# Score 1 moved beside the norms of a two-layer graph network kernel, and written into other PSUM banks

## The chip, the cores and the metric

The kernel runs on one core of a Trainium2 chip. The time is the device time of one execution in microseconds, from runs of the same program; the profile is of one execution. Engines are named as in the profile: PE is TensorE (matmul), DVE is VectorE, ACT is ScalarE, POOL is GpSimd, SP is SyncE, which here only issues DMAs.

## What is computed

128 graphs of 128 nodes with 512 features go through two layers, each with a residual and a normalisation ahead of it. The first layer weighs nodes by products of queries and keys, masked by the adjacency and divided by the norm of each row; the second is an attention with 8 heads of 64.

```python
    # layer 0
    q, k, v = h @ Wq.T, h @ Wk.T, h @ Wv.T
    rel = adjacency.T[None] * einsum('bnd,bmd->bnm', q, k)
    rel = rel / jnp.linalg.norm(rel, axis=2, keepdims=True)
    out = einsum('bnm,bmd->bnd', rel, v)
    # layer 1
    scores = einsum('bihd,bjhd->bhij', q, k) / sqrt(64)
    weights = softmax(scores + where(adj == 0, -1e9, 0), axis=-1)
    out = einsum('bhij,bjhd->bihd', weights, v)
    # around each layer
    h = maximum(layernorm(x), 0);  x = x + layer(h, adj, ...)
```

## The kernel before

The graphs are taken in 32 groups of four. One pass of the loop (g = 0 to 31) works on several groups at once: `m` is layer 0 of group g, `l` is layer 1 of group g - 1, `p` is layer 1 of the group before that, `f` is layer 0 of group g + 1 (loads, statistics, normalised rows), and `n` is layer 1 of group g being prepared. So each pass holds one whole layer 0 and one whole layer 1.

The order of everything is written by hand: strings of steps (`FIRST` for g = 0, `SECOND` for g = 1, `ORDER` for the 30 passes after, `LAST` behind the loop). A step such as `l.S1` calls the method `S(1)` of `l`. Each engine gets its instructions in the order in which the steps stand, and waits in that order; between engines only data dependencies and free buffers hold.

Steps that matter here:

- The linear maps are products of 512 x 512 matrices, each in seven smaller products (P1, P2, P5, P6, P3, P7, P4 in order of time) with sums of blocks in place of the eighth. Each small product is eight matmul instructions on PE (line 225) into one of three PSUM banks, called x, y and z. P1 writes x, and its result is copied out (r1). P2 writes y, and DVE adds r1 to it. P5 writes z (copied out as r5), P6 adds onto x (copied out as r2), P3 adds onto z, P7 onto x and P4 onto x again, each followed by an addition on DVE (line 249) or a copy. P3 may write z only when the copy of P5 has been read from it. In layer 0's V product the copies are on ACT; in layer 1's they add a bias on DVE (line 242).
- `m.R` (line 389) computes the four masked relations' products into an outputs' bank; `m.mask_rel` (DVE) multiplies them by the adjacency, `m.square` (ACT) squares them, `m.N` (PE, line 415) sums the squares with a matrix of ones, `m.norms` turns those sums by a transpose on DVE (line 424) and POOL takes the power -1/2. `m.O0` to `m.O3` (PE, line 429) multiply by the values, and `m.xO0` to `m.xO3` (DVE, line 435) scale by the norm and add to x.
- `l.S0` to `l.S3` (PE, line 460, with 64 rows of the array) compute the scores of the eight heads of one graph into `pss`, a pair of PSUM banks of which there is one. `l.mk` (DVE, lines 469 and 471) adds the mask and takes the negative maximum; `l.ex` (ACT, line 478) takes eight exponentials with sums and sends the block to DRAM on ACT's queue; `l.wr` fetches it back turned by blocks, four DMAs on SP's queue; `l.wt` (DVE, lines 491 and 493) takes a reciprocal and transposes inside the blocks. `l.A0` and `l.A1` (PE, line 577) multiply by the values.
- `n.stat` (DVE, lines 290 and 291) takes the statistics of x after layer 0, `n.inv` (POOL) turns them into scale and shift, `n.hn` (ACT, line 308) normalises and sends the rows to DRAM, `n.rd` (SP) fetches them, `n.T` (DVE, line 320) transposes: these are the inputs `h` of the next pass's products. `f.stat` and `f.inv` do the same for the next group's layer 0.

The PSUM pools: `ps_mm` has four banks for products, `ps_s` the one pair for scores, `ps_o` two banks with the tag `po` for outputs, for R and for N.

Of the kernel before, what the change touches and what calls it, by code (L numbers as in the profile page):

```python
# [9 lines left out]
F32 = mybir.dt.float32  # L10
AF = mybir.ActivationFunctionType
# [3 lines left out]
P = 128  # L15
G = 4
# [5 lines left out]
def kernel(  # L22
# [14 lines left out]
):  # L37
    nc = tc.nc
    B, N, D = x.shape
    assert N == P and B % G == 0  # L40
    KD = D // P
    H, HD = 8, 64
    NH = KD
    NG = B // G
# [8 lines left out]
    npool = ctx.enter_context(tc.tile_pool(name="npool", bufs=3))  # L53
# [3 lines left out]
    small = ctx.enter_context(tc.tile_pool(name="small", bufs=8))  # L57
# [4 lines left out]
    ps_s = ctx.enter_context(tc.tile_pool(name="ps_s", bufs=1, space=PSUM))  # L62
    ps_o = ctx.enter_context(tc.tile_pool(name="ps_o", bufs=2, space=PSUM))
# [122 lines left out]
    TB, BK = 4, 32  # L186

    def send_blocks(src, n: int, name: str):
        f = 8 * BK // n
        d = scratch.tile([n, P, TB, f], F32, tag=f"d{n}", name=f"d_{name}")  # L190
        nc.scalar.dma_start(d.rearrange("n p j f -> p n (j f)"), src.rearrange("p n j f -> p n (j f)"))
        return d
# [180 lines left out]
    class Layer0(Layer):  # L373
        n = 0

        def start(self):
            g = self.g
            self.gT = ppool.tile([P, KD, G * P], F32, tag="pgv", name=f"gT_{g}")
            self.v = ppool.tile([P, G, D], F32, tag="pv0", name=f"v0_{g}")
            self.po = {}  # L380
            self.G = Product(self, "a", self.gT, True, name=f"pg_{g}")
            self.V = Product(self, "v0", self.v, False, name=f"pv0_{g}")
# [27 lines left out]

        def N(self):

            pn = ps_o.tile([P, G, BK], F32, tag="po", name=f"pn_{self.g}")
            for c in range(TB):
                nc.tensor.matmul(
                    pn[c * BK : (c + 1) * BK, :, :], lhsT=ones, rhs=self.sq[:, c, :],
                    start=True, stop=True,
                )
            self.pn = pn

        def norms(self):
            self.rn = small.tile([P, G], F32, tag="rn", name=f"rn_{self.g}")
            sums = small.tile([P, G, BK], F32, tag="sums", bufs=1, name=f"sums_{self.g}")
            nc.vector.transpose(sums.rearrange("p b q -> p (b q)"), self.pn.rearrange("p b q -> p (b q)"))
            nc.gpsimd.tensor_tensor(self.rn, sums[:, :, 0], mhalf, ALU.pow)

        def O(self, b):
# [9 lines left out]
    class Layer1(Layer):  # L437
        n = 1

        def start(self):  # L440
            g = self.g
            self.qT = ppool.tile([P, NH, G * P], F32, tag="pq", name=f"qT_{g}")
            self.kT = ppool.tile([P, NH, G * P], F32, tag="pk", name=f"kT_{g}")
            self.Q = Product(self, "q", self.qT, True, bq_sb, name=f"pq_{g}")
            self.K = Product(self, "k", self.kT, True, bk_sb, name=f"pk_{g}")
            self.rs, self.wT, self.ps, self.nmax, self.po, self.e = {}, {}, {}, {}, {}, {}
            self.dw, self.uw, self.total, self.do, self.uo = {}, {}, {}, {}, {}

        def start_v(self):
# [3 lines left out]
        def S(self, b):  # L453
            g = self.g

            pss = ps_s.tile([P, 2, NH, P], F32, tag="ps", name=f"pss_{g}_{b}")
            for k in range(NH):
                for r in range(2):
                    rows = slice(r * HD, (r + 1) * HD)
                    nc.tensor.matmul(  # L460
                        pss[:, r, k, :],
                        lhsT=self.qT[rows, k, ts(b, P)], rhs=self.kT[rows, k, ts(b, P)],
                        start=True, stop=True,
                    )
            self.ps[b] = pss.rearrange("p r k j -> p (r k) j")

        def mk(self, b):
            g, sc = self.g, self.ps[b]
# [27 lines left out]
            )  # L496

        def mk_r(self, b, r):  # L500
            sc = self.ps[b][:, r * NH : (r + 1) * NH, :]
            nc.vector.tensor_tensor(sc, sc, mask[:, None, :].to_broadcast([P, NH, P]), ALU.add)
            if r == 0:
                self.nmax[b] = small.tile([P, H], F32, tag="nmax", bufs=2, name=f"nmax_{self.g}_{b}")
            nc.vector.tensor_reduce(
                self.nmax[b][:, r * NH : (r + 1) * NH], sc, AX.X, ALU.max, negate=True
            )
# [117 lines left out]
    SECOND = """  # L625
        l.Q.P1 l.sumA l.Q.P2 l.sumB l.K.P1 l.K.P2 l.Q.P5 l.Q.P6 f.load0 f.load1 l.Q.P3 l.K.P5 l.K.P6 l.Q.P7
        l.K.P3 l.K.P7 l.S0 l.mk0 f.load2 f.load3 l.Q.P4 l.K.P4 l.ex0 l.wr0 m.V.P1 f.stat0 f.stat1 f.inv0
        m.V.P2 l.S1 l.mk1 m.V.P5
        l.ex1 l.wr1 l.wt0 m.R m.mask_rel m.square f.stat2 f.stat3 f.inv1 m.V.P6 m.V.P3 m.N m.norms l.S2 l.mk2
        m.V.P7 l.ex2 l.wr2 l.wt1 m.O0 m.xO0 m.O1 m.xO1 n.stat0 n.stat1 n.inv0 m.V.P4 n.hn0 n.rd0 l.start_v l.V.P1  # L630
        m.O2 m.xO2 m.O3 m.xO3 n.stat2 n.stat3 n.inv1 l.V.P2 l.V.P5 n.hn1 l.V.P6 l.wt2
        n.rd1 l.V.P3 l.V.P7 n.T0 l.S3 l.A0 l.mk3 l.oc0 l.V.P4 l.ex3 n.T1 n.start
    """.split()
    ORDER = """
        l.Q.P1 p.rdo0 l.sumA l.Q.P2 p.wr3 m.hn0 l.sumB l.K.P1 m.rd0 l.K.P2 p.ot0 l.Q.P5 l.Q.P6 m.hn1 m.rd1
        l.Q.P3 l.Q.P7 p.wt3 m.T0 l.K.P5 l.K.P6 l.Q.P4 f.load0 f.load1 l.K.P3
        l.K.P7 m.T1 m.sumA m.sumB m.start m.G.P1 l.K.P4 m.G.P2 l.S0 p.A1 l.mk0 p.oc1 p.rdo1 m.G.P5 m.G.P6
        l.ex0 l.wr0 m.G.P3 m.V.P1 m.G.P7 p.ot1 m.V.P2 f.stat0 f.stat1 f.inv0 m.G.P4 l.S1 l.mk1 m.V.P5
        l.ex1 l.wt0 l.wr1 f.load2 f.load3 m.R m.mask_rel m.square m.V.P6 m.V.P3 m.N m.norms l.S2 l.mk2
        m.V.P7 l.ex2 l.wr2 l.wt1 m.O0 m.xO0 m.O1 m.xO1 n.stat0 n.stat1 n.inv0 m.V.P4 n.hn0 n.rd0 l.start_v l.V.P1  # L640
        m.O2 m.xO2 m.O3 m.xO3 n.stat2 n.stat3 n.inv1 l.V.P2 l.V.P5 n.hn1 f.stat2 f.stat3 f.inv1 l.V.P6 l.wt2
        n.rd1 l.V.P3 l.V.P7 n.T0 l.S3 l.A0 l.mk3 l.oc0 l.V.P4 l.ex3 n.T1 n.start
    """.split()
    LAST = """
# [19 lines left out]
    with tc.manual_schedule(engines={EN.PE, EN.SP, EN.Pool, EN.DVE, EN.Activation}):  # L664
        p, l, m = None, None, Layer0(0)
# [9 lines left out]
        f = Layer0(1)  # L675
# [3 lines left out]
        for g in range(NG):  # L679
            n = Layer1(g)  # L680
            if g:
                f = Layer0(g + 1) if g + 1 < NG else None
            run((FIRST, SECOND, ORDER)[min(g, 2)], p=p, l=l, m=m, n=n, f=f, w=Weights1())
            p, l, m = l, n, f
# [31 lines left out]
```

## Time and profile before

| | us |
|---|---|
| median of 3 runs | 2509.51 |
| lowest and highest | 2508.04, 2510.25 |
| the profiled execution | 2510.6 |
| its span | 2508.8 |
| ACT busy (share) | 1020.2 (41%) |
| exponentials, line 478, mean of one | 0.381 |
| mask and maximum over 1024, mean of one | 1.216 and 1.224 |
| transposes of weights, line 493, mean of one | 1.206 |
| statistics, line 290, mean of one | 0.671 |
| a score's matmuls, mean of one of 16 | 0.285 |
| TensorE clock granted | 0.999 |

The profiled execution is one of the same kind as the runs, with the span between its first and last instruction 1.8 us shorter than its time. "Mean of one" is an instruction's own length; instructions of one engine overlap at their ends, so the distance from start to start is shorter than that where they follow each other without a wait.

### The profile page before, as it was taken

Reading aid. Unit: us, or ns where it says so; the run is one execution under the profiler, and the core shown is the slowest. Engines: PE = TensorE matmul, PEld = TensorE weight load, DVE = VectorE, ACT = ScalarE, POOL = GpSimd, SP = SyncE. Lnnn points to the kernel's source line nnn. Section 1 sums busy time; section 2 is a strip of 40 time slices with the busy share of each in tenths; the row PEclk is TensorE's granted clock in tenths of the full one; section 3 lists DMA queues with packets and bytes.
Section 4 is the critical chain, followed back from the end, with each engine's and each line's share of the span. In section 5 each row is a group of like instructions: output and inputs, shape, how many; then the busy total and the mean of one; then the engine's idle time right before and its main releaser. Section 6 shows DMA issues by size and latency. Waiting matters only on the chain.

```text
span 2508.8 us, 40841 instructions
## 1 busy us (share of the span) xinstructions
PE 2488.8 (99%) x14672; PEld 2107.3 (84%) x14672; DVE 1709.0 (68%) x2485; ACT 1020.2 (41%) x3248; POOL 531.8 (21%) x944
## 2 busy tenths in 40 slices
PE   9999999999999999999999999999999999999998
PEld 6888888888888888888888888888888888888887
DVE  5566776666766667766677666676666776667766
ACT  3344343434434443434444343443443443444433
POOL 5111222121212212121122112121221212212211
PEclk9999999999999999999999999999999999999999
DMA  6255544555545555444555545554555644555543
GB/s 198 84 169 167 177 160 152 160 172 164 186 143 159 170 165 187 154 155 160 168 171 172 149 157 169 164 185 142 157 161 169 191 146 150 173 166 175 166 137 118
DMA packets 370475, 405.72 MB, mean 162 GB/s; under 512 B 29600, under 2 KB 286752, under 8 KB 370272
## 3 DMA queue, kind: packets, MB, share of 16 engines
q1 hardware_dynamic: 278992, 167.92, 24.8%
q10 hardware_dynamic: 70384, 166.74, 17.7%
q0 software_dynamic: 20896, 68.44, 8.3%
q8 instruction: 116, 1.90, 0.3%
q14 instruction: 87, 0.71, 0.1%
HBM read 204.80 MB, written 198.18 MB: 161 GB/s over the span
## 4 chain that ended last, share of the span: by engine, by line
PE 90%; DVE 4%; DMA 3%; ACT 1%; issue 1%; SPq 1%; POOL 0%; ACTq 0%; DVEq 0%
PE pv_x L225 15%; PE pg_x L225 9%; PE pk_x L225 8%; PE pq_x L225 8%; PE pv_z L225 8%; PE pss L460 5%; PE pg_z L225 5%; PE pq_z L225 5%; PE pr L389 4%; PE pk_z L225 4%; PE po L577 4%; PE pv_y L225 4%; PE po L429 4%; PE pg_y L225 2%; PE pk_y L225 2%; PE pq_y L225 2%
## 5 line engine op out<-in xcount | busy, mean ns | idle before, releaser
L478 ACT ACTIVATE e<-pss,nmax 128x128 f32<-128x128 f32 x1008 | 355.0, 381 | 281.3 <-PE pv_x L225 133.5
L612 POOL TENSOR_TENSOR xb<-xb,o 128x512 f32<-128x512 f32 x124 | 158.0, 1274 | 1212.6 <-DVE o L605 1211.1
L225 PE MATMUL pv_x<-wc_v,h 128*128 128x256 f32 x1280 | 301.6, 382 | 0.7 <-DVE pv_r L242 0.5
L225 PEld LDWEIGHTS pv_x<-wc_v,h 128*128 128x128 f32 x1280 | 239.4, 190 | 54.4 <-DVE v L249 11.7
L308 ACT ACTIVATE hn<-xb,shift,rstd 128x512 f32<-128x512 f32 x252 | 190.9, 807 | 172.5 <-POOL shift L300 170.6
L225 PE MATMUL pv_z<-wc_v,s 128*128 128x256 f32 x1024 | 245.1, 382 | 0.0
L320 DVE STREAM_TRANSPOSE h<-u_h 128x1024 f32<-128x1024 f32 x126 | 156.3, 1241 | 127.5 <-DMA u_h<-d_h 125.9
L478 ACT ACTIVATION_READ_ACCUMULATOR e<-pss,nmax 128x1 f32 x1008 | 221.2, 219 | 0.0
L225 PEld LDWEIGHTS pv_z<-wc_v,s 128*128 128x128 f32 x1024 | 191.8, 190 | 28.8
L225 PE MATMUL pv_x<-wc_v,s 128*128 128x256 f32 x768 | 184.9, 384 | 0.0
L225 PE MATMUL pq_x<-h,wc_q 128*128 128x256 f32 x768 | 181.9, 380 | 2.4 <-DVE h L320 2.4
L225 PE MATMUL pk_x<-h,wc_k 128*128 128x256 f32 x768 | 181.5, 379 | 0.0
L290 DVE BATCH_NORM_STATS2 st<-xb 128x6 f32<-128x512 f32 x256 | 171.9, 671 | 10.4 <-DMA xb<-in_x_dram 10.4
L588 ACT COPY oT<-po 128x512 f32<-128x512 f32 x124 | 72.7, 586 | 252.1 <-PE po L577 252.1
L493 DVE STREAM_TRANSPOSE wT<-u_w 128x1024 f32<-128x1024 f32 x126 | 151.9, 1206 | 32.6 <-DMA u_w<-d_w 32.6
L469 DVE TENSOR_TENSOR pss<-pss,mask 128x1024 f32<-128x1024 f32 x126 | 153.2, 1216 | 18.8 <-PE pss L460 15.0
L225 PEld LDWEIGHTS pq_x<-h,wc_q 128*128 128x128 f32 x768 | 145.3, 190 | 24.0 <-PE pv_x L225 2.1
L225 PEld LDWEIGHTS pk_x<-h,wc_k 128*128 128x128 f32 x768 | 145.8, 190 | 19.9
L225 PEld LDWEIGHTS pv_x<-wc_v,s 128*128 128x128 f32 x768 | 140.8, 190 | 20.6 <-issue 0.2
L460 PEld LDWEIGHTS pss<-kT,qT 64*128 64x128 f32 x2048 | 124.2, 187 | 39.4 <-issue 37.3
L471 DVE TENSOR_REDUCE nmax<-pss 128x8 f32<-128x1024 f32 x126 | 154.3, 1224 | 4.4
L460 PE MATMUL pss<-kT,qT 64*128 64x128 f32 x2048 | 148.7, 285 | 0.9 <-ACT e L478 0.5
(147 smaller groups left out, 4364.7 us busy)
## 6 DMA issues: line engine op xcount, KB each, us to landing
d_h<-hn ACTq DMA_DIRECT2D x126, 512.0 KB, 3.7
u_h<-d_h SPq DMA_DIRECT2D x504, 128.0 KB, 3.2
d_w<-e ACTq DMA_DIRECT2D x126, 512.0 KB, 2.6
u_w<-d_w SPq DMA_DIRECT2D x504, 128.0 KB, 3.0
xb<-in_x_dram POOLq DMA_DIRECT2D x124, 256.0 KB, 3.2
d_o<-oT ACTq DMA_DIRECT2D x62, 512.0 KB, 3.1
u_o<-d_o SPq DMA_DIRECT2D x248, 128.0 KB, 2.9
out_dram<-xb POOLq DMA_DIRECT2D x124, 256.0 KB, 3.1
```

Source lines behind the costliest of these rows:

```text
L225: nc.tensor.matmul(ps[:, m, :], lhsT=lhsT, rhs=rhs, start=first and m == 0 and k == 0, stop=k == 1, skip_group_check=True,)
L290: nc.vector.bn_stats(st, x_tiles[g, b])
L308: nc.scalar.activation(hn[:, r], x_tiles[g, b].rearrange("p (k j q) -> p j k q", j=TB, q=BK), AF.Relu, bias=self.shift[:, b : b + 1], scal ...
L320: nc.vector.transpose(half.rearrange("p k (t i) -> p t k i", i=BK), self.u.pop(i).rearrange("p t (k q) -> p t k q", q=BK),)
L389: nc.tensor.matmul(pr[:, b, :], lhsT=self.turned(k, b), rhs=self.gT[:, k, ts(b, P)], start=(k == 0), stop=(k == KD - 1),)
L429: nc.tensor.matmul(po, lhsT=self.rel[:, b, :], rhs=self.v[:, b, :], start=True, stop=True)
L460: nc.tensor.matmul(pss[:, r, k, :], lhsT=self.qT[rows, k, ts(b, P)], rhs=self.kT[rows, k, ts(b, P)], start=True, stop=True,)
L469: nc.vector.tensor_tensor(sc, sc, mask[:, None, :].to_broadcast([P, H, P]), ALU.add)
L471: nc.vector.tensor_reduce(self.nmax[b], sc, AX.X, ALU.max, negate=True)
L478: nc.scalar.activation(e[:, :, i, :], sc[:, i, :].rearrange("p (j q) -> p j q", q=BK), AF.Exp, bias=nmax[:, i : i + 1], accum_out=self.tot ...
L493: nc.vector.transpose(self.wT[b].rearrange("p h (t i) -> p t h i", i=BK), self.uw.pop(b).rearrange("p t (h q) -> p t h q", q=BK),)
L612: nc.gpsimd.tensor_tensor(xb, xb, o.rearrange("p k t q -> p (k t q)"), ALU.add)
```

## The change

Scores 1 (`S1`, in the passes that have a layer 0 beside them) no longer go to the pair `pss` but to two tiles of the outputs' pool `ps_o`, heads 0 to 3 of the kernel's order in one and 4 to 7 in the other. Mask, maximum and exponentials of scores 1 and 2 are done in halves: `mkA1`, `exC1`, `mkB1`, `exD1`, and the same for 2. `N` takes no outputs' bank any more, but the first part of the V product's bank y.

In the order, `S1` moves from ahead of `m.V.P5` to between `m.V.P6` and `m.N`, with `S2` behind `N`; R comes earlier by that much; `m.V.P3` moves behind `S2`. `wt0` stands ahead of R without a score before it. `wr1` is issued later, `wt1` goes from ahead of `xO0` to behind `xO3`. In `ORDER`, `f.stat2` moves to ahead of `l.V.P1` and `f.stat3` to ahead of `l.V.P2`; before, both stood behind `l.V.P5`.

```diff
         def N(self):
-            pn = ps_o.tile([P, G, BK], F32, tag="po", name=f"pn_{self.g}")
+            pn = self.V.ps["y"].rearrange("p m (b q) -> p (m b) q", q=BK)[:, 0:G, :]
...
         def S(self, b):
-            pss = ps_s.tile([P, 2, NH, P], F32, tag="ps", name=f"pss_{g}_{b}")
+            if b == 1 and g < NG - 1:
+                half = [ps_o.tile([P, NH, P], F32, tag="po", name=f"pso_{g}_{r}") for r in range(2)]
+            else:
+                pss = ps_s.tile([P, 2, NH, P], F32, tag="ps", name=f"pss_{g}_{b}")
+                half = [pss[:, r] for r in range(2)]
+                self.ps[b] = pss.rearrange("p r k j -> p (r k) j")
+            self.half_s[b] = half
...
-                        pss[:, r, k, :],
+                        half[r][:, k, :],
...
+        def ex_h(self, b, r):
+            g, sc, nmax = self.g, self.half_s[b][r], self.nmax[b]
+            if r == 0:
+                self.total[b] = small.tile([P, H], F32, tag="total", bufs=4, name=f"total_{g}_{b}")
+                self.e[b] = npool.tile([P, TB, H, BK], F32, tag="e", name=f"e_{g}_{b}")
+            e = self.e[b]
+            for k in range(NH):
+                i = r * NH + k
+                nc.scalar.activation(
+                    e[:, :, i, :], sc[:, k, :].rearrange("p (j q) -> p j q", q=BK), AF.Exp,
+                    bias=nmax[:, i : i + 1], accum_out=self.total[b][:, i : i + 1],
+                )
+            if r == 1:
+                self.dw[b] = send_blocks(self.e.pop(b).rearrange("p j h q -> p (j h q)").rearrange(
+                    "p (n j f) -> p n j f", n=1, j=TB), 1, f"w_{g}_{b}")
...
         def mk_r(self, b, r):
-            sc = self.ps[b][:, r * NH : (r + 1) * NH, :]
+            sc = self.half_s[b][r]
...
     ORDER = """
...
-        l.ex0 l.wr0 m.G.P3 m.V.P1 m.G.P7 p.ot1 m.V.P2 f.stat0 f.stat1 f.inv0 m.G.P4 l.S1 l.mk1 m.V.P5
-        l.ex1 l.wt0 l.wr1 f.load2 f.load3 m.R m.mask_rel m.square m.V.P6 m.V.P3 m.N m.norms l.S2 l.mk2
-        m.V.P7 l.ex2 l.wr2 l.wt1 m.O0 m.xO0 m.O1 m.xO1 n.stat0 n.stat1 n.inv0 m.V.P4 n.hn0 n.rd0 l.start_v l.V.P1
-        m.O2 m.xO2 m.O3 m.xO3 n.stat2 n.stat3 n.inv1 l.V.P2 l.V.P5 n.hn1 f.stat2 f.stat3 f.inv1 l.V.P6 l.wt2
+        l.ex0 l.wr0 m.G.P3 m.V.P1 m.G.P7 p.ot1 m.V.P2 f.stat0 f.stat1 f.inv0 m.G.P4 m.V.P5
+        l.wt0 f.load2 f.load3 m.R m.mask_rel m.square m.V.P6 l.S1 m.N l.S2 l.mkA1 m.norms l.exC1 l.mkB1 l.exD1
+        l.wr1 m.V.P3 l.mkA2 l.exC2 m.V.P7 l.mkB2 l.exD2 l.wr2 m.O0 m.xO0 m.O1 m.xO1 n.stat0 n.stat1 n.inv0
+        m.V.P4 n.hn0 n.rd0 l.start_v f.stat2 l.V.P1 m.O2 m.xO2 m.O3 m.xO3 l.wt1 n.stat2 n.stat3 n.inv1 f.stat3
+        f.inv1 l.V.P2 l.V.P5 n.hn1 l.V.P6 l.wt2
         n.rd1 l.V.P3 l.V.P7 n.T0 l.S3 l.A0 l.mk3 l.oc0 l.V.P4 l.ex3 n.T1 n.start
     """.split()
```

`SECOND` changes in the same way, but keeps `f.stat2 f.stat3 f.inv1` ahead of `m.V.P6`.

More of the change, by code (lines that the diff above doesn't have):

```diff
@@ L416, in N @@
                     pn[c * BK : (c + 1) * BK, :, :], lhsT=ones, rhs=self.sq[:, c, :],
-                    start=True, stop=True,
+                    start=True, stop=True, skip_group_check=True,
                 )
-            self.pn = pn
         def norms(self):
@@ L423, in norms @@
             sums = small.tile([P, G, BK], F32, tag="sums", bufs=1, name=f"sums_{self.g}")
-            nc.vector.transpose(sums.rearrange("p b q -> p (b q)"), self.pn.rearrange("p b q -> p (b q)"))
+            nc.vector.transpose(sums.rearrange("p b q -> p (b q)"), self.V.ps["y"].rearrange("p m h -> p (m h)")[:, 0:P])
             nc.gpsimd.tensor_tensor(self.rn, sums[:, :, 0], mhalf, ALU.pow)
@@ L446, in start @@
             self.rs, self.wT, self.ps, self.nmax, self.po, self.e = {}, {}, {}, {}, {}, {}
+            self.half_s = {}
             self.dw, self.uw, self.total, self.do, self.uo = {}, {}, {}, {}, {}
@@ L464, in S @@
                     )
-            self.ps[b] = pss.rearrange("p r k j -> p (r k) j")
         def mk(self, b):
@@ L496, in wt, with exC, exD @@
             )
+        def ex_h(self, b, r):
[13 more added lines that the diff above has]
+                    "p (n j f) -> p n j f", n=1, j=TB), 1, f"w_{g}_{b}")
+        def exC(self, b):
+            self.ex_h(b, 0)
+        def exD(self, b):
+            self.ex_h(b, 1)
         def mk_r(self, b, r):
-            sc = self.ps[b][:, r * NH : (r + 1) * NH, :]
+            sc = self.half_s[b][r]
             nc.vector.tensor_tensor(sc, sc, mask[:, None, :].to_broadcast([P, NH, P]), ALU.add)
@@ L627 @@
         l.K.P3 l.K.P7 l.S0 l.mk0 f.load2 f.load3 l.Q.P4 l.K.P4 l.ex0 l.wr0 m.V.P1 f.stat0 f.stat1 f.inv0
-        m.V.P2 l.S1 l.mk1 m.V.P5
-        l.ex1 l.wr1 l.wt0 m.R m.mask_rel m.square f.stat2 f.stat3 f.inv1 m.V.P6 m.V.P3 m.N m.norms l.S2 l.mk2
-        m.V.P7 l.ex2 l.wr2 l.wt1 m.O0 m.xO0 m.O1 m.xO1 n.stat0 n.stat1 n.inv0 m.V.P4 n.hn0 n.rd0 l.start_v l.V.P1
-        m.O2 m.xO2 m.O3 m.xO3 n.stat2 n.stat3 n.inv1 l.V.P2 l.V.P5 n.hn1 l.V.P6 l.wt2
+        m.V.P2 m.V.P5 l.wt0 m.R m.mask_rel m.square f.stat2 f.stat3 f.inv1 m.V.P6 l.S1 m.N l.S2 l.mkA1 m.norms l.exC1
+        l.mkB1 l.exD1 l.wr1 m.V.P3 l.mkA2 l.exC2 m.V.P7 l.mkB2 l.exD2 l.wr2 m.O0 m.xO0 m.O1 m.xO1 n.stat0 n.stat1
+        n.inv0 m.V.P4 n.hn0 n.rd0 l.start_v l.V.P1 m.O2 m.xO2 m.O3 m.xO3 l.wt1 n.stat2 n.stat3 n.inv1 l.V.P2
+        l.V.P5 n.hn1 l.V.P6 l.wt2
         n.rd1 l.V.P3 l.V.P7 n.T0 l.S3 l.A0 l.mk3 l.oc0 l.V.P4 l.ex3 n.T1 n.start
@@ L637 @@
         l.K.P7 m.T1 m.sumA m.sumB m.start m.G.P1 l.K.P4 m.G.P2 l.S0 p.A1 l.mk0 p.oc1 p.rdo1 m.G.P5 m.G.P6
-        l.ex0 l.wr0 m.G.P3 m.V.P1 m.G.P7 p.ot1 m.V.P2 f.stat0 f.stat1 f.inv0 m.G.P4 l.S1 l.mk1 m.V.P5
-        l.ex1 l.wt0 l.wr1 f.load2 f.load3 m.R m.mask_rel m.square m.V.P6 m.V.P3 m.N m.norms l.S2 l.mk2
-        m.V.P7 l.ex2 l.wr2 l.wt1 m.O0 m.xO0 m.O1 m.xO1 n.stat0 n.stat1 n.inv0 m.V.P4 n.hn0 n.rd0 l.start_v l.V.P1
-        m.O2 m.xO2 m.O3 m.xO3 n.stat2 n.stat3 n.inv1 l.V.P2 l.V.P5 n.hn1 f.stat2 f.stat3 f.inv1 l.V.P6 l.wt2
+        l.ex0 l.wr0 m.G.P3 m.V.P1 m.G.P7 p.ot1 m.V.P2 f.stat0 f.stat1 f.inv0 m.G.P4 m.V.P5
[3 more added lines that the diff above has]
+        f.inv1 l.V.P2 l.V.P5 n.hn1 l.V.P6 l.wt2
         n.rd1 l.V.P3 l.V.P7 n.T0 l.S3 l.A0 l.mk3 l.oc0 l.V.P4 l.ex3 n.T1 n.start
```

## The prediction

> **What bounds the kernel now.** I read the page's first two parts, then the waits of TensorE, then the order of time on PE and DVE in one group of the loop.
>
> ```profile
> span 2508.8 us, 40841 instructions
> PE 2488.8 (99%) x14672; PEld 2107.3 (84%) x14672; DVE 1709.0 (68%) x2485; ACT 1020.2 (41%) x3248; POOL 531.8 (21%) x944
> PE pq_x L225 <- DVE h L320: 2.4, 3, 1.1
> PE pv_x L225 <- DVE pv_r L242: 0.5, 3, 0.2
> ```
>
> TensorE sets the end: 99% busy, almost nothing waited for. The other engines count only where they come late for one of its steps. Ends on PE are modelled, so I measure its steps from start to start. A product of eight matmuls takes 1.727 us wherever nothing disturbs it. Compared with the shortest time of the same step, all starts of the trace together hold 11.2 us of excess: some 10 us of it in the loop, at three places: Q.P1 waiting for `h`, Q.P5 for the addition behind Q.P2, and V.P7 of layer 1 for its bias copy on DVE. A group without a wait lasts 76.73 us (N to N), the mean one 77.1.
>
> This is PE in the pass g = 15 (the first columns are start and length):
>
> ```profile
> 1177.03 1.16 PE L460 MATMUL pss<-kT,qT 64*128 64x128 f32 x16
> 1178.12 1.99 PE L225 MATMUL pv_z<-wc_v,s 128*128 128x256 f32 x8
> 1179.95 3.73 PE L389 MATMUL pr<-gT,h 128*128 128x128 f32 x32
> 1183.52 1.89 PE L225 MATMUL pv_x<-wc_v,s 128*128 128x256 f32 x8
> 1185.25 1.89 PE L225 MATMUL pv_z<-wc_v,s 128*128 128x256 f32 x8
> 1187.07 0.43 PE L415 MATMUL pn<-sq,ones 128*32 128x128 f32 x8
> 1187.43 1.16 PE L460 MATMUL pss<-kT,qT 64*128 64x128 f32 x16
> 1188.52 1.99 PE L225 MATMUL pv_x<-wc_v,s 128*128 128x256 f32 x8
> 1202.42 1.89 PE L225 MATMUL pv_z<-wc_v,s 128*128 128x256 f32 x8
> 1204.45 1.99 PE L225 MATMUL pv_x<-wc_v,h 128*128 128x256 f32 x8
> ```
>
> The reader should see two things. V.P5 after S1 takes 1.83 us to the next start, V.P3 before N 1.82, both instead of 1.727: going to a narrow form costs 0.09 and coming back 0.10, while N to S2 costs nothing. And V.P7 of layer 1 (last line) starts 2.03 after V.P3: 0.31 of waiting. DVE shows for what:
>
> ```profile
> 1188.64 1.23 DVE L469 TENSOR_TENSOR pss<-pss,mask 128x1024 f32<-128x1024 f32 x1 [0.47 <-PE pss L460]
> 1193.38 1.25 DVE L493 STREAM_TRANSPOSE wT<-u_w 128x1024 f32<-128x1024 f32 x1 [1.55 <-DMA u_w<-d_w]
> 1194.55 1.36 DVE L435 SCALAR_TENSOR_TENSOR xb<-po,rn,xb 128x512 f32<-128x512 f32 x2
> 1201.52 0.68 DVE L242 TENSOR_TENSOR pv_r<-pv_z,bv_sb 128x512 f32<-128x512 f32 x1
> 1203.73 0.66 DVE L242 TENSOR_TENSOR pv_r<-pv_x,bv_sb 128x512 f32<-128x512 f32 x1
> ```
>
> From S2 on DVE runs without a break, but for 1.55 us before wt1, where it waits for a DMA. The copy of V.P6 starts at 1203.73 and PE goes on at 1204.45, 0.72 later. The copy of V.P5, at 1201.52, was due by 1202.42 - 0.72 = 1201.70 for V.P3. This queue has little to spare, and the change works on it.
>
> [...] The trace: a mask and maximum over 1024 takes 1.26 + 1.14 = 2.40 us from start to start; in the last stage, where they go in halves, 0.73 + 0.61 = 1.34, so two halves 2.68: 0.14 for each instruction added.
>
> **The change, part by part.**
>
> *Narrow steps together.* One pair of switches goes in each of the 31 groups that have a layer 1: 31 x 0.197 = 6.1 us off. S1 to N isn't in the trace; N to S2 and S0 to the outputs of layer 1 (64*128 to 128*64) show no cost, so 0, at most another 0.1 (3 us).
>
> *R, and S1 in the outputs' banks.* Without S1 ahead and its switches, V.P6 would start at 1183.52 - 1.09 - 0.20 = 1182.23, S1 at 1184.05, N 1185.14, S2 1185.50, V.P3 1186.59, V.P7 1188.42; from O0 on all is 0.20 earlier. S1's second bank is that of R, free when mask_rel has read it: R ends at 1182.2, mask_rel takes 0.7, and wt0 ahead of it has its data 7.2 us after ex0's issue at 1171.93, so 1179.2. S1 waits for nothing, by over 1 us. N in V's y bank: y was read at 1177.6, the square is done near 1183.8. O0 and O1 need the halves read by exC1 and exD1, about 1188.0 and 1189.6, against 1190.15. S2 no longer waits for score 1 at all. Cost 0.
>
> *Halves.* Two more instructions for each of two scores on DVE, 0.28 each. ACT does the same exponentials, 0.34 us apart.
>
> *DVE up to V.P5's copy.* V.P3's addition can't start before its product ends: 1186.59 + 2.03 = 1188.62 (a product's addition starts 1.93 after the product, 0.10 more behind a score). By then mkA1, norms, mkB1 are done (1185.12 + 1.34 + 0.22 + 1.34 = 1188.02). From there nothing is waited for: V.P3's addition 0.61, mkA2 1.34, V.P7's addition 0.60, mkB2 1.34: xO0 at 1192.51 (before 1194.55). xO0, xO1 1.29; two statistics of n 1.61; f.stat2, new here, 0.81; V.P1's copy 0.57; xO2, xO3 1.32; wt1 0.11 + 1.12; two statistics 1.61; f.stat3, new here, 0.81; V.P2's addition 0.57. Sum from xO0: 9.82, so V.P5's copy starts at 1202.33. PE could start V.P3 at 1202.22 and gets it at 1202.33 + 0.72 = 1203.05: **a new wait of 0.83**, and 0.10 more, as the step after each such wait in the trace is 0.104 longer. 29 groups have an f in this order: 29 x 0.93 = 27.0 us. In the group run by SECOND, f's statistics stand elsewhere, and the last has no f: 1.6 us less on DVE, no wait.
>
> *wt1 later.* Its data: mkB1 done 1188.1, exD1 until 1189.6, issue about 1189.75, last block 7.28 later (median of this trace; longest 11.7): 1197.0, turn at 1198.2. Now this fetch runs beside score 2's writing; the fourth weights, which share the DMA, take 8.6. So 0 to 0.4 of wait in a typical group; I take 0.05, 1.5 us. On SP, wr1 and wr2 go ahead of rd0: wr2's issue is at about 1194.1, as before; rd0 needs hn0, 2 us earlier than before. rd0 also needs the buffer that wt1 frees, at 1199.3, before hn0's rows have landed (1202.4). Cost 0.
>
> *Waits that go.* hn0 comes 2 us earlier, so h, mk3, ex3 and Q's copies do too, against 0.6 more time on PE. The largest wait for h is 1.21, for qT 0.36. V.P7's goes, since its copy follows V.P5's by 0.6. I take 9.5 of 10 us off.
>
> Sum: -6.1 + 27.0 + 1.5 - 9.5 = **+12.9 us**. The profiled execution took 2510.6 around its span of 2508.8, the median run 2509.5: 2522.
>
> **Rivals.** (a) *DVE comes in time*: the copy of V.P5 is 0.83 earlier than I add up, or V.P3 doesn't wait for it. For it: xO0 is 2 us earlier, and this wait isn't in the trace before. Against: V.P7 waits for a copy in the same way, and every duration is measured. It gives 2509.5 - 6.1 - 9.5 = 2494. It decides for a faster kernel where the wait is below 0.2 us. (b) *The sum is right and wt1 comes late as well*: DVE has no slack left, so each 0.1 us of DMA delay costs 2.9 us; with 0.6 instead of 0.05, 2538. (c) *Half the wait*: 0.4 instead of 0.83, if additions start earlier than I take it; 2509.5 - 6.1 - 9.5 + 29 x 0.5 + 1.5 = 2510, no change. Slower by what can be told begins at a wait of 0.56.
>
> **Numbers.** Forecast, slower by a wait at layer 1's V.P3: 0.62 (2514.6 to 2534). (b) 0.13. (c) 0.09. (a) 0.16. What a measurement of this kernel can tell from no change is 0.2%, 5 us. Faster 0.16, same 0.09, slower 0.75. The likeliest's own range, from waits of 0.5 to 1.3, is 2511 to 2535; the range 2505 to 2535 takes in (c) and leaves (a) and the far part of (b) out.
>
> **What would show it.** Right: S1, N, S2 in a row with V.P6's next start at 1.82 and V.P3's at 1.83; a wait of PE for `pv_r` (L242) before `pv_z` in nearly every group; none left for `h` and `qT`; xO0 5.9 us behind V.P3's start. Wrong: no such wait, or one ended by a DMA before wt1, or PE waiting before S1 or the outputs.

## The result and the profile after

| | before | after |
|---|---|---|
| median, us (5 runs each) | 2509.04 | 2567.50 |
| lowest and highest | 2507.39, 2510.25 | 2563.59, 2568.77 |
| ratio, 95% interval | 1 | 1.0231 [1.0220, 1.0243] |
| profiled execution, its span | 2510.6, 2508.8 | 2563.6, 2561.8 |
| a pass of the loop, N to N, median of 29 | 76.91 | 78.65 |

The change makes the kernel 2.3% slower: 58 us, where 12.5 was forecast (2522 against 2509.5). The direction is right, the size is wrong, and the time lies outside the forecast's range.

First the page of the kernel after:

```profile
span 2561.8 us, 40938 instructions
PE 2493.8 (97%) x14672; PEld 2107.2 (82%) x14672; DVE 1727.8 (67%) x2609; ACT 1030.2 (40%) x3248; POOL 531.5 (21%) x944
```

And its waits of TensorE (who waits for whom: us in total, times, longest):

```profile
PE po L429 <- ACT v L233: 27.9, 32, 1.1
PE pv_z L225 <- DVE pv_r L242: 21.8, 29, 1.3
...
PE pso L467 <- DVE rel L398: 2.3, 1, 2.3
```

TensorE's busy time has hardly changed; two waits have appeared that stand in nearly every pass, and one that stands in one pass. The second of these lines is the forecast one: V.P3 of layer 1 waiting for V.P5's bias copy, 29 times. The first was not forecast: O2 waiting for ACT's copy of V.P4. This is one pass on PE (g = 14; start and length first, the wait in brackets):

```profile
1130.76 1.89 PE L225 MATMUL pv_x<-wc_v,s 128*128 128x256 f32 x8
1132.58 1.16 PE L467 MATMUL pso<-kT,qT 64*128 64x128 f32 x16
1133.67 0.43 PE L416 MATMUL pv_y<-sq,ones 128*32 128x128 f32 x8
1134.03 1.16 PE L467 MATMUL pss<-kT,qT 64*128 64x128 f32 x16
1135.12 1.99 PE L225 MATMUL pv_z<-wc_v,s 128*128 128x256 f32 x8
...
1140.40 3.62 PE L225 MATMUL pv_x<-wc_v,h 128*128 128x256 f32 x16
1144.87 1.98 PE L429 MATMUL po<-v,rel 128*128 128x512 f32 x4 [0.86 <-ACT v L233]
...
1152.74 1.99 PE L225 MATMUL pv_z<-wc_v,s 128*128 128x256 f32 x8 [0.70 <-DVE pv_r L242]
```

S1, N and S2 stand in a row and cost what they should: 1.82 from V.P6 to S1, 1.09 and 0.36 between them, nothing for S1 to N, 1.83 from V.P3 to V.P7. From V.P4's start to O2's are 4.47 us where two products take 3.45: a wait of 1.02. The bracket says 0.86, because it counts from the modelled end; I keep to starts. V.P3 waits 0.86 by its start. What comes before O2 is on DVE and ACT:

```profile
1135.35 0.67 DVE L530 TENSOR_TENSOR pso<-pso,mask 128x512 f32<-128x512 f32 x1
1136.05 0.69 DVE L533 TENSOR_REDUCE nmax<-pso 128x4 f32<-128x512 f32 x1
...
1137.83 0.69 DVE L530 TENSOR_TENSOR pss<-pss,mask 128x512 f32<-128x512 f32 x1
...
1139.16 0.68 DVE L249 TENSOR_TENSOR v<-pv_x,pv_r 128x512 f32<-128x512 f32 x1
1140.87 0.70 DVE L530 TENSOR_TENSOR pss<-pss,mask 128x512 f32<-128x512 f32 x1 [1.03 <-ACT e L513]
1142.21 1.40 DVE L435 SCALAR_TENSOR_TENSOR xb<-po,rn,xb 128x512 f32<-128x512 f32 x2
...
1152.00 0.68 DVE L242 TENSOR_TENSOR pv_r<-pv_z,bv_sb 128x512 f32<-128x512 f32 x1
```

The second half of score 1, `pso` at 1135.35, goes on while ACT takes the exponentials of the first (from 1135.28). The second half of score 2, `pss` at 1140.87, waits 1.03 us for the exponentials of its first half. The halves of score 1 are two tiles, those of score 2 two halves of one. On ACT, score 1 (first line) and score 2:

```profile
1136.33 0.38 ACT L513 ACTIVATE e<-pso,nmax 128x128 f32<-128x128 f32 x1
...
1140.37 0.37 ACT L513 ACTIVATE e<-pss,nmax 128x128 f32<-128x128 f32 x1
...
1142.33 0.37 ACT L513 ACTIVATE e<-pss,nmax 128x128 f32<-128x128 f32 x1 [1.49 <-DVE nmax L533]
...
1143.87 0.33 ACTq L191 DMA_DIRECT2D d_w<-e  x1
1144.23 0.59 ACT L233 COPY v<-pv_x 128x512 f32<-128x512 f32 x1 [0.40 <-PE pv_x L225]
```

ACT idles 1.49 us in the middle of score 2, does four exponentials and issues a DMA, and only then copies V.P4, whose product ended near 1142.1 (V.P4 starts at 1140.40, a product takes 1.73). O2 starts at 1144.87, when that copy is done, 0.64 behind the copy's start. In the kernel before, in the pass of the prediction, the copy stood behind exponentials and a DMA issue too, but started 0.95 ahead of O2 (1195.52):

```profile
1194.57 0.59 ACT L233 COPY v<-pv_x 128x512 f32<-128x512 f32 x1 [0.45 <-ACT e L478]
```

So it had about 0.3 us to spare there.

The maxima of both halves (`nmax`) also lie in one tile, in SBUF and in columns of their own. There nothing is serialised: DVE writes those of score 1's second half from 1136.05, while ACT still reads the first half's for its last exponential at 1136.33. So a shared tile does not always make a wait; here it was the two-bank tile in PSUM (the 1.03 us above).

The third wait is the one of the pass g = 1. On DVE:

```profile
106.76 1.25 DVE L499 STREAM_TRANSPOSE wT<-u_w 128x1024 f32<-128x1024 f32 x1 [5.79 <-DMA u_w<-d_w]
107.93 0.65 DVE L398 TENSOR_TENSOR rel<-pr,adj_sb 128x512 f32<-128x512 f32 x1
```

And on PE:

```profile
108.64 1.16 PE L467 MATMUL pso<-kT,qT 64*128 64x128 f32 x14 [2.27 <-DVE rel L398]
```

In `SECOND` wt0 comes sooner behind ex0, DVE waits 5.79 us for its data, mask_rel stands behind it, and the second bank of S1 is still R's: PE stops after the first two matmuls of S1.

An account of PE's starts over the whole profiled executions, each step's time to the next start against the shortest time of the same step:

| | forecast, us | measured, us |
|---|---|---|
| narrow steps together, 31 x 0.197 | -6.1 | -6.1 |
| V.P3 for V.P5's copy, 29 passes, with the longer step behind | +27.0 | +29.5 |
| of that, wt1's data late | +1.5 apart | within the 29.5 |
| old waits (11.2 before; 3.5 left) | -9.5 | -7.7 |
| O2 for V.P4's copy, 31 x 1.04 and 31 x 0.10 | 0 | +35.5 |
| S1 in the pass g = 1 | 0 | +2.8 |
| sum | +12.9 | +54.0 |

The spans differ by 53.0. Nearly all of the error stands in one line, that of O2. This tells where TensorE stood still; what each cause is worth, the experiments tell.

### The profile page after: what moved, and what is told of

Its sections match the earlier page's. It is cut to its first block, busy times and chain, and to the rows that moved or that the text cites. A ratio compares the mean times of both kernels' runs of the same rounds, so it can differ in the third digit from the quotient of the medians.

```text
span 2561.8 us, 40938 instructions
## 1 busy us (share of the span) xinstructions
PE 2493.8 (97%) x14672; PEld 2107.2 (82%) x14672; DVE 1727.8 (67%) x2609; ACT 1030.2 (40%) x3248; POOL 531.5 (21%) x944
## 4 chain that ended last, share of the span: by engine, by line
PE 78%; DVE 14%; ACT 3%; DMA 2%; issue 2%; SPq 0%; DVEq 0%; POOL 0%; ACTq 0%
PE pg_x L225 9%; PE pv_x L225 9%; PE pk_x L225 8%; PE pq_x L225 8%; PE pv_z L225 7%; PE pg_z L225 5%; PE po L605 4%; PE pq_z L225 4%; PE pr L389 4%; PE pk_z L225 4%; PE pss L467 4%; DVE st L290 4%; DVE xb L435 3%; PE pv_y L225 2%; PE pg_y L225 2%
## 5 line engine op out<-in xcount | busy, mean ns | idle before, releaser
L484 ACT ACTIVATE e<-pss,nmax 128x128 f32<-128x128 f32 x512 | 180.3, 383 | 43.7 <-DVE nmax L477 33.9
L429 PE MATMUL po<-v,rel 128*128 128x512 f32 x256 | 123.6, 605 | 27.9 <-ACT v L233 27.9
L633 DVE TENSOR_TENSOR o<-o,rs 128x512 f32<-128x512 f32 x124 | 124.5, 1004 | 4.3
L297 POOL TENSOR_SCALAR rstd<-mv 128x2 f32<-128x2 f32 x128 | 28.4, 222 | 465.6 <-DVE mv L291 460.9
L225 PE MATMUL pg_z<-s,wc_a 128*128 128x256 f32 x512 | 124.1, 385 | 0.0
L225 PE MATMUL pq_z<-s,wc_q 128*128 128x256 f32 x512 | 121.4, 380 | 1.4 <-DVE qT L249 1.4
```

The lines of the kernel that those rows point to most:

```text
L225: nc.tensor.matmul(ps[:, m, :], lhsT=lhsT, rhs=rhs, start=first and m == 0 and k == 0, stop=k == 1, skip_group_check=True,)
L429: nc.tensor.matmul(po, lhsT=self.rel[:, b, :], rhs=self.v[:, b, :], start=True, stop=True)
L484: nc.scalar.activation(e[:, :, i, :], sc[:, i, :].rearrange("p (j q) -> p j q", q=BK), AF.Exp, bias=nmax[:, i : i + 1], accum_out=self.tot ...
L633: nc.vector.tensor_tensor(heads, heads, self.rs.pop(b).rearrange("p (r k) -> p k r", r=2)[:, :, :, None].to_broadcast([P, NH, 2, HD]), ALU ...
```

## The experiments

Two theories. **A**: mkB2's wait for exC2, made by the tile that the halves share, delays exD2 and the copy and so O2; V.P3's wait is DVE's queue; the two lie on linked chains. **B**: ACT is late by itself (halves, the copy's place), and each wait adds its own time. Ratios are to the kernel before, run beside them on the same chip; its median there was 2506.4 to 2507.1.

**1. Tiles of their own for the halves.**

```diff
-                pss = ps_s.tile([P, 2, NH, P], F32, tag="ps", name=f"pss_{g}_{b}")
-                half = [pss[:, r] for r in range(2)]
+                half = [ps_s.tile([P, NH, P], F32, tag=f"ps{r}", name=f"pss_{g}_{b}_{r}") for r in range(2)]
```

> The two halves of every score lie in two PSUM tiles of one bank each instead of one tile of two banks (scores 0 and 3 therefore also take mask and maximum in halves, 0.28 us more on DVE each). Theory A (mkB2 on DVE waits 1.03 us for the exponentials exC2 only because both halves are one tile; this makes exD2 and the copy behind V.P4 late and O2 waits 1.02 + 0.10 us on PE): the wait of DVE before the second half of score 2 goes, O2's wait goes, V.P3's wait of 0.86 stays, because PE and DVE both come 1.1 us earlier; 31 x 1.12 = 35 us less, about 2533. Theory B (ACT is late by itself, with halves and the copy's place in its queue): O2 still waits, at least 0.7 us, and the time stays above 2550.

Measured 2538.4, ratio 1.0124 [1.0109, 1.0140]. In one pass DVE takes the second half of score 2 and xO0 without a wait:

```profile
1056.41 0.69 DVE L526 TENSOR_TENSOR pss<-pss,mask 128x512 f32<-128x512 f32 x1
...
1057.74 1.40 DVE L435 SCALAR_TENSOR_TENSOR xb<-po,rn,xb 128x512 f32<-128x512 f32 x2
```

xO0 starts 7.42 us behind N instead of 8.54, O2 waits for nothing, and a pass has a median of 77.53 us instead of 78.65. V.P3's wait stays at 0.80. That is theory A, and B is out: ACT has the same exponentials and copies in the same order and is in time. The typical pass gains the 1.12 us that were forecast, but the whole gains 27 us by the ratios and not 35. The mean of the passes is 77.97: with DVE earlier wt1's data come 1.2 to 2.1 us late in four of them, and in three places behind waits of 1.96 us or more TensorE's granted clock is 0.50, for 13.7 us in all, with 0.996 in the mean of the execution (last section). The wait of 1.03 came from the tile: with the order as it was and a half to each bank in both kernels, the edit takes it to zero.

**2. f.stat2 and f.stat3 back behind l.V.P5**, as before the change.

```diff
-        m.V.P4 n.hn0 n.rd0 l.start_v f.stat2 l.V.P1 m.O2 m.xO2 m.O3 m.xO3 l.wt1 n.stat2 n.stat3 n.inv1 f.stat3
-        f.inv1 l.V.P2 l.V.P5 n.hn1 l.V.P6 l.wt2
+        m.V.P4 n.hn0 n.rd0 l.start_v l.V.P1 m.O2 m.xO2 m.O3 m.xO3 l.wt1 n.stat2 n.stat3 n.inv1
+        l.V.P2 l.V.P5 n.hn1 f.stat2 f.stat3 f.inv1 l.V.P6 l.wt2
```

> Only f.stat2 and f.stat3 go back behind l.V.P5, as in the kernel before; all else is the changed kernel. Theory A (V.P3's wait is DVE's queue, which these two made 1.62 us longer ahead of V.P5's copy): the wait of 0.86 + 0.10 at V.P3 goes in all 29 passes, O2's wait stays at 1.02, so 28 us less, about 2539. Rival (the copy is late because of the wait before mkB2 alone, or because wt1's data are late): V.P3 still waits, and less than 10 us is gained.

Measured 2551.2, ratio 1.0177 [1.0162, 1.0192]; a pass takes 78.04. V.P3's standing wait is gone (3 times left), O2's is the same to 0.01. But 14 us are gained by the ratios, not 28: V.P7 now waits 0.263 in 30 passes, with 0.104 for the step behind it, for V.P6's copy, which these statistics now precede. These 11 us are most of what is missing; the wait moved by one product, and I had overlooked that end.

**3. exD2 behind V.P4's copy.**

```diff
-... l.mkB2 l.exD2 l.wr2 m.O0 ... m.V.P4 n.hn0
+... l.mkB2 m.O0 ... m.V.P4 l.exD2 l.wr2 n.hn0
```

> Only exD2 and wr2 go behind V.P4's copy in the order, so that the copy no longer stands behind them on ACT. Theory A (DVE's queue from V.P3's addition to V.P5's copy sets the pass, and O2's wait lies inside it): O2's wait of 1.02 goes and V.P3's grows from 0.86 to about 2.0; the time stays at 2567 within 4 us. Theory B (the two waits are independent and add up): 31 x 1.12 = 35 us less, about 2533.

Measured 2562.5, ratio 1.0224 [1.0208, 1.0239], where the changed kernel had 1.0231: the same. A pass takes 78.64, as before this edit. The waits of TensorE in this run:

```profile
PE pv_z L225 <- DVE pv_r L242: 53.3, 31, 1.8
...
PE po L429 <- ACT v L233: 0.7, 1, 0.7
```

O2's wait is left in one pass of 32, and V.P3's has grown to 1.98 by its starts (1.8 by the modelled ends, as this view counts). The largest wait of the profile was removed and nothing came of it, since DVE's queue from V.P3's addition to V.P5's copy sets the pass, and O2's wait lay inside that time. The two waits don't add up.

**4. Both: tiles of their own, and the statistics behind l.V.P5.**

> Tiles of their own for the halves, and f.stat2 and f.stat3 back behind l.V.P5. Theory A: both waits go (O2 is covered by about 0.1 us, V.P3 by 0.7), a pass lasts 76.53 us, the gain of 6.1 us for the narrow steps and the 9.5 us of old waits remain: 2494, from 2490 to 2500, faster than before. Theory B: O2's wait stays, 2525 or more.

Measured 2525.0, ratio 1.0078 [1.0062, 1.0095]: a miss. Both waits are gone from the typical pass, but it takes 76.99 and not 76.53: V.P7's wait of 0.267 is here too, in 29 passes. And with DVE 1.1 us earlier, wt1's data come late in some passes: five have a wait of V.P3 again, 1.6 us in the median.

**5. exC2 behind mkB2**, the tiles as in the changed kernel.

> Only exC2 goes behind mkB2 in the order, ahead of exD2; the tiles are those of the changed kernel. Theory A (mkB2 waits for exC2 because it stands behind it and both touch one tile): no wait of DVE inside score 2, xO0 1.1 us earlier as with tiles of their own, but all eight exponentials start only then, so O2 waits 1.35 + 0.10 us for the copy and V.P3 no longer waits; a pass lasts 77.98 us instead of 78.65, about 20 us less, 2547. Rival (mkB2 waits for something else of ACT or PE): the wait before mkB2 stays near 1 us and xO0 isn't earlier.

Measured 2563.1, ratio 1.0229 [1.0213, 1.0244]; a pass takes 78.71. DVE in one pass:

```profile
1142.23 0.69 DVE L530 TENSOR_TENSOR pss<-pss,mask 128x512 f32<-128x512 f32 x1
...
1143.56 1.40 DVE L435 SCALAR_TENSOR_TENSOR xb<-po,rn,xb 128x512 f32<-128x512 f32 x2
...
1148.84 1.61 DVE L435 SCALAR_TENSOR_TENSOR xb<-po,rn,xb 128x512 f32<-128x512 f32 x2 [0.89 <-PE po L429]
```

Inside score 2 nothing is waited for any more, with the shared tile in place: it takes both, the exponentials of one half ahead of the mask of the other in the order, and one PSUM tile for both. O2 waits 1.35, as expected. The forecast of the time failed on the last line: xO2 waits 0.89 for O2, so DVE gives back most of what it had gained, and V.P3 still waits 0.60. This is the link between the two waits: O2 late makes xO2 late, and V.P5's copy stands behind xO2 on DVE.

**6. The kernel before with the later turn of wt1 alone** (behind xO3).

> The kernel before with one part of the change alone: wt1 goes from ahead of xO0 to behind xO3. If the later turn is a gain by itself, DVE's wait of about 1 us for wt1's data goes, xO0 starts 1.1 to 2.3 us earlier, the waits of PE for h and for the copies of V.P6 go, and 5 to 9 us are gained (2500 where before is 2509). If the old waits come from DMA delays of another kind (rows of h fetched late), less than 3 us are gained.

Measured 2510.7, ratio 1.0017 [1.0010, 1.0024]: slightly slower, where 5 to 9 us less were forecast. The waits for `h` and `qT` are gone, so they did come from wt1's wait; but wt1 now always stands ahead of V.P6's copy, and V.P7 waits 0.264 in 30 passes instead of up to 0.35 in some.

**7. The changed kernel with wt1 back ahead of xO0.**

> The changed kernel with wt1 back ahead of xO0. Score 1's block is sent at 1138.4 in the pass that ends near 1160 and needs 7.2 us to come back, DVE reaches wt1 at 1142.2. If the later turn is needed with the later exponentials, DVE waits 3.3 us there in every pass, O2 (its bank is freed by xO0) waits about 3.6 us in place of 1.0, V.P3 about 1.6; a pass lasts 81.9 us instead of 78.65, 100 us more: 2668, or more still if PE's clock falls in waits of this length. If the turn doesn't matter, 2567 as it is.

Measured 2683.2, ratio 1.0705 [1.0690, 1.0719]. A pass takes 82.04, O2 waits 3.73: as worked out. With the exponentials of score 1 so late, the later turn is needed. The mean of the passes is 82.64, and the 15 us beyond the forecast lie in the few passes that are longer than the median; TensorE's granted clock is 0.50 in stretches at these waits, and 0.974 to 0.976 in the mean of each execution (last section).

**8. A version that loses no time.** It is made in three runs, called b1, b2 and b5 in the texts below. First the statistics go behind l.V.P6's copy, ahead of wt2, with tiles of their own (b1); then also wt1 behind n.stat3 (b2); then also wt0 of the pass g = 1 behind wr1 (b5).

> Tiles of their own, and f.stat2 and f.stat3 behind l.V.P6's copy instead of ahead of it. In the run with tiles of their own and the statistics behind l.V.P5 the wait left in each pass was 0.267 + 0.104 us at V.P7, for V.P6's copy behind these statistics. If that is all, 29 x 0.37 = 10.8 us less than that run's 2525: about 2514. If wt1's data then come late or T0 falls behind (statistics ahead of it), less than 5 us.

> As the run b1, and wt1 goes behind n.stat3. In the run with tiles of their own and the statistics behind l.V.P5 five passes lost 1.1 to 1.9 us because wt1's data came late; wt1 1.6 us later takes most of that away: 5 to 9 us less than b1, about 2507. If the fetch of h, which needs wt1's buffer, then comes later, Q.P5's wait for qT grows instead and nothing is gained.

> As the run b2, and in the order of the second pass (g = 1) wt0 goes from ahead of R to behind wr1. In that pass b2's DVE waits 6.1 us for wt0's data, mask_rel stands behind it, and PE waits 2.6 us in the middle of S1, after which its clock was at half for 6.8 us. If both are due to wt0's place, they go: 3 us of wait and some 3 us of clock, 2498. If the clock falls there anyway, 2501.

Measured 2514.1 (ratio 1.0035 [1.0021, 1.0049]), 2503.9 (0.9990 [0.9981, 0.9998]) and 2500.2 (0.9975 [0.9966, 0.9984]). Each came within 4 us of its number. The pass is 76.62 from the first on. The second removes late data of wt1, 10 us where 5 to 9 were forecast; the third removes the wait in the pass g = 1, of 2.60 us, and the 6.8 us behind it in which the granted clock was 0.50. The last version is faster than both kernels.

**9. Is that due to the change?** The kernel before with the two moves of order alone (called b6 below):

```diff
-        m.V.P7 l.ex2 l.wr2 l.wt1 m.O0 m.xO0 m.O1 m.xO1 n.stat0 n.stat1 n.inv0 m.V.P4 n.hn0 n.rd0 l.start_v l.V.P1
-        m.O2 m.xO2 m.O3 m.xO3 n.stat2 n.stat3 n.inv1 l.V.P2 l.V.P5 n.hn1 f.stat2 f.stat3 f.inv1 l.V.P6 l.wt2
+        m.V.P7 l.ex2 l.wr2 m.O0 m.xO0 m.O1 m.xO1 n.stat0 n.stat1 n.inv0 m.V.P4 n.hn0 n.rd0 l.start_v l.V.P1
+        m.O2 m.xO2 m.O3 m.xO3 n.stat2 n.stat3 n.inv1 l.wt1 l.V.P2 l.V.P5 n.hn1 l.V.P6 f.stat2 f.stat3 f.inv1 l.wt2
```

> The kernel before (score 1 where it was, whole scores, N in an outputs' bank) with the two moves of order of the run b5 alone: wt1 behind n.stat3, and f.stat2 and f.stat3 behind l.V.P6. If these moves make b5 faster than before, this one loses its old waits as well: a pass of 76.73 us without waits, 6 to 10 us less than before (2497 to 2501), and the narrow steps put together are worth the rest, up to 6 us. If the moves need the rest of the change, it isn't faster than before by 3 us.

> The kernel of the run b5, on the chip of the run b6 for the comparison: 6 us less than before as in its first run. By PE's steps it should be 0.197 us a pass, 6 us in all, ahead of b6 if both lose all waits; its pass was 76.62 us where 76.53 is possible, so 3 us are left of that.

Measured 2500.0, ratio 0.9973 [0.9962, 0.9984], and for the version of 8 beside it 2499.8, ratio 0.9971 [0.9960, 0.9983]. They can't be told apart. DVE in the kernel before with the two moves:

```profile
1187.57 0.68 DVE L249 TENSOR_TENSOR v<-pv_x,pv_r 128x512 f32<-128x512 f32 x1
1188.17 1.40 DVE L435 SCALAR_TENSOR_TENSOR xb<-po,rn,xb 128x512 f32<-128x512 f32 x2
...
1192.25 0.69 DVE L242 TENSOR_TENSOR pv_r<-pv_x,bv_sb 128x512 f32<-128x512 f32 x1 [1.07 <-PE pv_x L225]
...
1199.14 0.69 DVE L242 TENSOR_TENSOR pv_r<-pv_x,bv_sb 128x512 f32<-128x512 f32 x1 [0.40 <-PE pv_x L225]
```

xO0 follows V.P7's addition at once, and both bias copies of V.P1 and V.P6 wait for PE, no longer PE for them. A pass takes 76.75, the mean over the loop is 76.77; in the other version the median is 76.62 and the mean 76.76. So the narrow steps still bring 0.13 us in the typical pass, and a few late passes take it back (waits for `h` in six, 3.1 us together by starts; the kernel with the two moves has one, of 0.2). That the fuller queue of DVE makes these passes late is a guess of mine; no run shows it.

## Why the prediction was wrong in size

Point by point, by its own steps:

- **Narrow steps together**: right, 0.197 a pass, and S1 to N free, as taken.
- **"R, and S1 in the outputs' banks ... Cost 0"**: right in `ORDER`. It was worked out for that string alone; in `SECOND` wt0's data are not there when its turn comes, which cost TensorE 2.8 us.
- **"Halves. Two more instructions for each of two scores on DVE, 0.28 each"**: this is the step that failed. The instructions are priced right (1.34 a half). But they were compared only with the last stage, where both masks stand ahead of both exponentials, and a wait of one half's mask for the other half's exponentials was put at nothing, without a reason. In score 1 it is nothing; in score 2 it is 1.03 us, as runs 1 and 5 showed. "From there nothing is waited for" holds with tiles of their own: there xO0 came 7.42 behind N, and by the prediction's times 7.37; in the changed kernel it came 8.54 behind.
- **The copy of V.P4**: no term stood for it. On my own times exD2 and the DMA issue would have left it ready just when O2 needs it, without cover; the sum gave O0 and O1 a check, O2 none. So 1.03 us on DVE became 1.02 us on PE, 35.5 us in all. Run 1 took the cause away and gained 1.12 us a pass, 27 us in the whole. Run 3 shows that the copy's place by itself is worth nothing while DVE is late.
- **V.P5's copy and V.P3's wait**: right. 0.83 was worked out, and 0.80 measured in run 1, where the other wait is gone. That the changed kernel itself shows 0.86 is in part luck: DVE came 1.17 us later than worked out and TensorE 1.12, and the two nearly cancel. The 0.10 for the step behind it and the 29 passes are right too.
- **wt1 later**: right in kind; most passes have the data in time, three lost 0.4 to 0.6 more.
- **Waits that go**: 7.7 of the 9.5, net of what stays. In the version without standing waits some for `h` came back.
- **The range**: its ends, 2511 and 2535, leave out the 1.5 us for wt1's data that the sum has. This changes nothing here.

Rival (a), in which DVE comes in time, is out; (b), at 2538, is out as well: the data of wt1 were in time in most passes. So is (c): the wait is not half of what was worked out. Of the prediction's own signs of being wrong, "PE waiting before S1 or the outputs" is the one that came, at O2 in every pass; and xO0 came 7.09 us behind V.P3's start, not 5.9.

## What to carry to other kernels

When an operation is split in two halves so that two engines overlap, look at what the program takes the halves to be: here the second half's write followed the first half's read in the order, and one PSUM tile of two banks serialised them (DVE waited 1.03 us in the pass shown), while two tiles did not (no wait in run 1). The largest wait of a profile is not a price: remove it alone and see whether it moves to the next consumer of the same queue, as it did here without a change in time. And a copy that frees a bank belongs in its queue ahead of statistics that are needed only later: this was worth 11 us from run 4 to the first version of run 8, and with the later turn of wt1 it took 7 us off the kernel before, where the rearranged matmuls added nothing that could be told.

## What the runs showed of the hardware

In the run with wt1 early TensorE's granted clock is 0.50 for part of each pass with a long wait of PE. PE at one wait:

```profile
369.51 3.56 PE L429 MATMUL po<-v,rel 128*128 128x512 f32 x4 [3.55 <-DVE xb L435]
```

And the stretch of it by engines (length, busy time of PE, weight loads, DVE, ACT and POOL, then the granted clock, the DMA share and GB/s):

```profile
369.70:373.10 3.40, 3.40 (x5) 1.34 (x5) 3.29 (x9) 0.00 (x0) 1.17 (x3) 0.50 0.53 149
```

O2 and O3 take 3.56 us there, against 1.98 in the pass g = 14 of the changed kernel. In all 31 passes with such a wait, of 3.48 us or more, the granted clock is 0.50 for a stretch of 3.41 us (26 times) or twice that (5 times), which begins up to 1.3 us after the wait's end or some time before it. Of the 29 waits in run 3, 1.82 to 1.84 us long, none was followed by that. Of those of 1.95 to 2.91 us in all runs together, seven were and seven were not, the single wait in the pass g = 1 among both kinds (2.27 us in the kernel after was not, 2.60 us in the second version of run 8 was). The shortest that was followed is one of 1.96 us, in run 1. What makes waits of like length differ, no run here shows. These lengths count from the modelled ends, so that the waits of 1.82 are those of 1.98 by their starts.

In run 1 the longer executions are those with the lower mean clock, over 6 us (2534.2 at 0.998, 2540.4 at 0.996); run 2 doesn't keep to this (2550.8 at 0.997, 2553.8 at 0.998). The executions of the last version of run 8, and of the kernel of run 9, lie within 2.6 us each at 0.998 or 0.999. Times differ at one clock too: the 30 runs of the kernel before beside runs 5, 6 and 8 differ by 6 us, all at 0.999. The kernel after has two executions at 0.999, 2563.6 (the profiled one) and 2564.7, and three at 0.997 to 0.998, of 2567.5 and more; its median lies 4 us above the profiled execution.
